# Mamba, attention and expert layers on one core: whole-row accumulations, a fifth slot for the products with B, gate column sums later

## Chip, cores and metric

The kernel runs on one core of one Trainium2 chip. The metric is the device time of a launch in microseconds (us), lower is better; the median of several runs counts.

## What is computed

The input is an image batch of 8 x 256 x 32 x 32, read as 8 sequences of 1024 tokens with 256 channels. Layer 0 is a Mamba block with a feed-forward part; layer 1 is attention with eight heads and a column bias from edges, then a mixture of experts; all in float32. What this case touches is the selective scan of layer 0 (d_inner 512, 16 states):

```python
xz = x @ W_in
xm, z = jnp.split(xz, 2, axis=-1)
...
xm = jax.nn.silu(xm)
dbl = xm @ W_x
dt, Bm, Cm = jnp.split(dbl, [dt_rank, dt_rank + d_state], axis=-1)
dt = jax.nn.softplus(dt @ W_dt + b_dt)
A = -jnp.exp(A_log)
def step(h, inputs):
    dt_t, B_t, C_t, x_t = inputs
    dA = jnp.exp(dt_t[..., None] * A)
    h = dA * h + (dt_t * x_t)[..., None] * B_t[:, None, :]
    y = jnp.einsum('bds,bs->bd', h, C_t)
    return (h, y)
...
y = ys.transpose(1, 0, 2) + xm * D_param
y = y * jax.nn.silu(z)
return y @ W_out
```

## The kernel before, in words

Each of the 8 sequences is cut into two chunks of 512 tokens, so there are 16 chunks, numbered 0 to 15. Even numbers are first chunks of a sequence (state zero at the start), odd ones are second chunks. The program is written as Python generators that emit instructions for the engines: TensorE (PE), VectorE (DVE), ScalarE (ACT), GpSimd (POOL) and SyncE (SP, which issues most DMAs). Every engine runs its own instructions in the order in which they were emitted.

The backbone is the loop at lines 2018 to 2051. It goes over 16 chunks x 32 steps = 512 groups. A group is one of 16 states (s) and one half (h, 256 of the 512 inner channels). For a group

- `decay` (line 763) has ScalarE compute exp(dt * A) into `da_all`, two groups ahead;
- `inputs` (line 780) takes a slot of `h4` and has DVE multiply x * dt by the row of B: hb, 128 x 1024;
- `scan` (line 791) has DVE run the recurrence along the tokens: one scan of 1024 in a first chunk (the decay of the second row's first column is set to zero), two of 512 with a starting state in a second chunk. In a first chunk POOL then copies the last column into `state`;
- `sums` (line 814) has DVE multiply hb by the row of C, and POOL issues a DMA that adds hb to the accumulator `dx` (`me["acc", h]`), which began as x * D. The slot comes free when that DMA has landed. In a first chunk multiply and DMA leave out the last column, because POOL's copy may still be reading it.

`h4` is a set of four slots (`H4` at line 263) of 4 KB a partition. The class `Slots` (line 275) hands out the slot that comes free first by the planner's own clock; the machine then waits for the true landing.

Around the backbone other streams are emitted by `advance` (line 1908), in an order of urgency: `prologue(i)` (line 561: load, layer norm, input product, convolution, dt), `park` (line 829: for chunks 2 to 15, layer norm and the gate z, both stored to DRAM), `gate_part` (line 852: brings silu(z) of a chunk back, as `sz`), `epilogue` (line 900: the gated y, the output product, the feed-forward part), then attention and the experts. `Model` (line 62) and the cost functions (lines 102 to 120) keep a running clock for each engine while the program is being written, and a stream is continued when its clock says that what it waits for is ready. `keep_warm` (line 1894) puts small filler products on PE where the model finds it idle. Tables give the moment of each start: `FRONT[i]` is the step of chunk i at which the prologue of i + 1 starts, `GATE[i]` that of its gate part; `CONV` and `SOFT` choose between forms of the convolution and of softplus (with `SOFT` 1, ScalarE and one more accumulating DMA do what a DVE instruction does otherwise; it doesn't act on chunk 0).

W_in is held as one tile `w_in` with 1024 columns: the first 512 give x, the rest z. `fold` (line 456) multiplies the columns by the layer norm's gain and makes the column sums of its shift. It is called for the x half in the head (line 1993), and for the z half by `setup` (line 1951), whose first piece is emitted at line 1991 while the loads are being issued.

At the end of a first chunk its last column has no term from C, since `sums` left it out. `epilogue` (lines 911 to 922) makes that term from `state` and C of the last token, and adds it to the accumulator's last column, ahead of the wait for the last accumulation to land (line 924).

Of the kernel before, what the change touches and what calls it, by code (L numbers as in the profile page):

```python
# [9 lines left out]
F32 = mybir.dt.float32  # L10
# [3 lines left out]
ALU = mybir.AluOpType  # L14
AX = mybir.AxisListType
PSUM = bass.MemoryType.PSUM

P = 128
B, C, L = 8, 256, 1024
KC = C // P  # L20
CH = 512
NCH = L // CH
DI, NS, RK, KW = 512, 16, 16, 4
ND = DI // P
HID = 1024
NH, HD = 8, 32
NPAIR = NH // 2
NHALF = ND // 2
# [26 lines left out]
def hybrid_kernel(ctx: ExitStack, tc: tile.TileContext, a: dict, out: bass.AP):  # L55
# [21 lines left out]
    model = Model()  # L77
# [58 lines left out]
    def load(name, shape, src):  # L136
        t = const.tile(shape, F32, name=name, tag=name)
        loads.append((t, src))
        return t
# [4 lines left out]
    def V(name, i=None, n=1):  # L144
        lo, hi = VEC[name]
        return vecs[:, lo:hi] if i is None else vecs[:, lo + i : lo + i + n]

    work = ctx.enter_context(ExitStack())
    work.enter_context(tc.manual_schedule(engines=set(ENGINES)))
    w_in = load("w_in", [P, KC, 2 * DI], a["W_in"].rearrange("(k p) n -> p k n", p=P))  # L150

    w_x = const.tile([P, ND, 4 * RK], F32, name="w_x")
    w_dt = const.tile([3 * RK, NHALF, P], F32, name="w_dt")
# [61 lines left out]
    taps = const.tile([P, ND * KW, HD], F32, name="taps")  # L215
    vec.memset(conv_tail, 0.0)
    b_in = const.tile([P, 2 * ND], F32, name="b_in")
    b1 = const.tile([P, HID // P], F32, name="b1")

    state = const.tile([P, NS, ND], F32, name="state")  # L220
    xsum = const.tile([P, KC, B, NCH], F32, name="xsum")
# [41 lines left out]
    T4, H4, PT, AHEAD, LAG, TICK = 25, 4, 4, 2, 8.0, 0.15  # L263


    FRONT = (7, 1, 1, 1, 1, 10, 16, 3, 14, 1, 10, 1, 13, 1, 13)
    GATE = (20, 7, 29, 25, 29, 21, 20, 15, 18, 30, 25, 28, 25, 14, 26, 15)
    CONV = (0, 0, 1, 1, 1, 1, 0, 0, 0, 0, 0, 0, 0, 0, 0, 0)
    SOFT = (0, 1, 1, 1, 1, 1, 0, 0, 0, 1, 0, 1, 1, 0, 1, 0)

    POLL, PARK = -1.0, 2
# [182 lines left out]
    def fold(w, n, gain, shift, bias, name, first=0):  # L456


        ps = sbank(f"{name}_{first}")
        cols = slice(first * P, (first + n) * P)  # L460
        for o in range(n):
            for k in range(KC):
                pe.matmul(
                    ps[:, o : o + 1], w[:, k, cols][:, o * P : (o + 1) * P], V(shift, k),
                    start=(k == 0), stop=(k == KC - 1),
                )
        yield
        if name == "b1":
            vec.tensor_tensor(bias, ps[:, :n], V("b1"), ALU.add)
        else:  # L470
            vec.tensor_copy(bias[:, first : first + n], ps[:, :n])
        for k in range(KC):
            vec.tensor_scalar(w[:, k, cols], w[:, k, cols], V(gain, k), None, ALU.mult)
# [87 lines left out]
    def prologue(i: int):  # L561
# [25 lines left out]
        def skip_path():  # L587

            for h in range(NHALF):
                dx = me["acc", h] = yield from mem.take(f"dx_{i}_{h}")  # L590
                for r in range(2):
                    act.activation(
                        dx[:, r, :], xm[h][:, r, :], AF.Identity, scale=V("D", 2 * h + r)
                    )

        if i == 0:
            yield from skip_path()
# [160 lines left out]
    def place(g):  # L758
        i, k = divmod(g, NSTEP)
        s, h = divmod(k, NHALF)  # L760
        return i, s, h
# [18 lines left out]
    def inputs(g):  # L780

        i, s, h = place(g)
        hb = hbs[g] = h4.now(f"hb_{g}")
        bc, landed = bcs[g // NHALF]
        vec.at = max(vec.at, landed)
        xd = chunk[i]["xd"][h]
        vec.tensor_tensor(hb, xd, bc[:, 0, :].unsqueeze(1).to_broadcast([P, 2, CH]), ALU.mult)
        if s == NS - 1:
            t4.put(xd)
# [24 lines left out]
    def sums(g):  # L814

        i, s, h = place(g)
        me = chunk[i]
        bc, _ = bcs[g // NHALF] if h < NHALF - 1 else bcs.pop(g // NHALF)
        hb = hbs.pop(g)
        n = CH if i % NCH == NCH - 1 else CH - 1  # L820
        y = hb[:, :, :n]
        vec.tensor_tensor(y, y, bc[:, 1, :n].unsqueeze(1).to_broadcast([P, 2, n]), ALU.mult)
        model.t = vec.at
        me["landed", h] = pool.dma_start(out=me["acc", h][:, :, :n], in_=y, accum_op=ALU.add)
        h4.put(hb, at=me["landed", h])

    parked = {}
# [1 line left out]
    def park():  # L829

        for i in range(PARK, B * NCH):
            b, c = divmod(i, NCH)
            xn_d = dram.tile([P, KC, CH], F32, name=f"xn_d_{i}", tag=f"xn_d_{i}")
            sz_d = dram.tile([NHALF, P, 2, CH], F32, name=f"sz_d_{i}", tag=f"sz_d_{i}")
            mem = Owner(t4, 3)
            xn = yield from mem.take(f"xe_{i}")
            yield sp.dma_start(xn, x_v[b, :, :, c * CH : (c + 1) * CH])
            yield from layernorm(mem, banks, xn, xn, f"a{i}")
            yield
            stored = sp.dma_start(xn_d, xn)  # L840
            sz = yield from gates(i, mem, xn)
            mem.put(xn, at=max(stored, model.end))
            for t in sz:
                act.activation(t, t, AF.Silu)
            lnexp()
            yield
            for h in range(NHALF):
                mem.put(sz[h], at=sp.dma_start(sz_d[h], sz[h]))
            mem.end()
            parked[i] = xn_d, sz_d  # L850

    def gate_part(i):

# [22 lines left out]
    def gates(i, mem, xn):  # L876

        while not gates_ready:
            yield POLL
        sz, ps = [], None  # L880
        for d in range(ND + 1):
            if d:
                h, q = divmod(d - 1, 2)
                act.activation(
                    sz[h][:, q, :], ps, AF.Identity, bias=b_in[:, ND + d - 1 : ND + d]
                )
                banks.put(ps)
            if d < ND:
                if d % 2 == 0:
                    sz.append((yield from mem.take(f"sz_{i}_{d // 2}")))  # L890
                ps = yield from banks.take(f"z_{i}_{d}")
                for k in range(KC):
                    pe.matmul(
                        ps, w_in[:, k, DI + d * P : DI + (d + 1) * P], xn[:, k, :],
                        start=(k == 0), stop=(k == KC - 1),
                    )
                yield
        return sz

    def epilogue(i: int):  # L900
# [9 lines left out]
        y = me["sz"]  # L910
        if c < NCH - 1:
            for h in range(NHALF):
                yl = work_pool.tile([P, NS + 1, 2], F32, name=f"yl_{i}_{h}", tag="yl")
                vec.tensor_tensor(
                    yl[:, 1:], state[:, :, 2 * h : 2 * h + 2],
                    me["c_last"].unsqueeze(2).to_broadcast([P, NS, 2]), ALU.mult,
                )
                vec.tensor_reduce(
                    yl[:, 0], yl[:, 1:].rearrange("p s d -> p d s"), AX.X, ALU.add
                )  # L920
                y_end = me["acc", h][:, :, CH - 1]
                vec.tensor_tensor(y_end, y_end, yl[:, 0], ALU.add)
        for h in range(NHALF):
            yield me["landed", h]
            vec.tensor_tensor(y[h], me["acc", h], y[h], ALU.mult)
            t4.put(me["acc", h])
        yield
# [932 lines left out]
    with tc.tile_pool(name="work", bufs=1) as work_pool:  # L1860
# [81 lines left out]
        def setup():  # L1942
            mem = Owner(t4, 9)
            tiles = []
            for n in range(9):
                tiles.append((yield from mem.take(f"setup_{n}")))
            held = []
            for n in range(2):
                held.append((yield from pairs.take(f"setup_p{n}")))
            pl = Scratch([t4.of[id(t)][1] for t in tiles])  # L1950
            yield from fold(w_in, ND, "ln1_g", "ln1_b", b_in, "b_in", ND)
            gates_ready.append(True)
            yield
            yield from column_bias(pl)
            yield
            eye = pl.tmp("eye", [P, P], F32)
            make_identity(nc, eye)
            blk = pl.tmp("eye_b", [P, HD], F32)
            yield
            for r in range(4):  # L1960
                rows = slice(HD * r, HD * r + HD)
                vec.tensor_copy(blk[rows, :], eye[rows, rows])
            vec.tensor_tensor(
                taps, blk.unsqueeze(1).to_broadcast([P, ND * KW, HD]),
                V("conv_w").unsqueeze(2).to_broadcast([P, ND * KW, HD]), ALU.mult,
            )
            set_up.append(True)
            yield
            yield from fold(w1, HID // P, "ln2_g", "ln2_b", b1, "b1")
            yield  # L1970
            yield from bounds(pl)
            yield
            yield from values_bias(pl)
            expert_constants(pl)
            mem.put(*tiles)
            mem.end()
            pairs.put(*held)
# [9 lines left out]
        next(first)  # L1987
        for n, (t, src) in enumerate(loads):
            sp.dma_start(t, src)
            if n == 2:  # L1990
                next(second)

        folding = fold(w_in, ND, "ln1_g", "ln1_b", b_in, "b_in")
        for n in range(8):
# [324 lines left out]
```

## Time and profile before

| what | value |
|---|---|
| median of 3 runs | 3440.32 us (3433.74 to 3444.18) |
| the profiled execution's own time | 3450.06 us |
| its span in the profile | 3448.1 us |
| DVE busy | 3031.7 us (88%) |
| PE busy | 3192.0 us (93%), filler included |
| ACT busy | 2459.8 us (71%) |
| accumulations of hb | 512 DMAs of 512 or 511 KB |
| DMA queue 0 (issued by POOL) | 138176 packets, 371.52 MB, 57.7% of 16 engines |

The profile names groups of instructions by what they write and read: `hb<-xm,bc` is the product with B, `hb<-da_all,hb` and `hb<-da_all,state,hb` are the scans, `hb<-hb,bc` is the product with C, `dx<-hb` is the accumulating DMA. Nearly all instructions carry line 98, the place where the planner emits them, so groups are told apart by their tiles. "Idle before" is time in which the engine stood still ahead of the instruction, with what ended it. DVE and ACT times can be added up; PE's busy time contains pipelined products.

### The profile page before, as it was taken

To read this page: it belongs to the slowest core of one execution; us is meant where nothing else is said; L and a number is where in the kernel's file an instruction comes from. 1 tells how busy PE (TensorE), PEld (TensorE's weight loads), DVE (VectorE), ACT (ScalarE), POOL (GpSimd) and SP (SyncE) were. 2 spreads that over 40 slices of the span, in tenths; PEclk is the share of its full clock that TensorE was granted. 3 is DMA by queue.
4 is the path that set the end of the run, shared out by engine and by line. 5 is a ranking of instruction groups with operands and counts; after the bars stand their busy time and mean duration, and the time that the engine had idled before them with its cause. 6 is when DMAs were issued, how large, how long until landed. Compare 5 with 4: busy or idle time off the path is not lost. (4 is left out here: it accounts for less than half of the span.)

```text
span 3448.1 us, 40234 instructions
## 1 busy us (share of the span) xinstructions
PE 3192.0 (93%) x14371; PEld 1355.8 (39%) x14371; DVE 3031.7 (88%) x3171; ACT 2459.8 (71%) x3550; POOL 1127.5 (33%) x1068
## 2 busy tenths in 40 slices
PE   7888889899999999999999998999999999999997
PEld 4544343433343334333443334334433343334343
DVE  5889999999999899999999999999999999972561
ACT  4665857578777887887778876887778768764643
POOL 0243224322542244233452244325542243311010
PEclk9889999899999999999999999999999999999999
DMA  3878999989998999898998989799889989971120
GB/s 105 222 170 204 213 224 214 226 206 228 196 206 185 210 203 218 181 210 198 228 207 188 221 196 222 187 215 207 193 189 209 202 191 199 225 160 61 32 77 23
DMA packets 233187, 642.22 MB, mean 186 GB/s; under 512 B 29520, under 2 KB 106000, under 8 KB 232976
## 3 DMA queue, kind: packets, MB, share of 16 engines
q0 software_dynamic: 138176, 371.52, 57.7%
q1 hardware_dynamic: 94800, 268.03, 23.5%
q8 instruction: 115, 1.88, 0.2%
q14 instruction: 96, 0.79, 0.1%
HBM read 253.33 MB, written 77.07 MB: 96 GB/s over the span
## 5 line engine op out<-in xcount | busy, mean ns | idle before, releaser
L95 POOL DMA_DIRECT2D dx<-hb x512 | 540.5, 1059 | 1567.2 <-DVE hb L98 1127.5
L98 ACT ACTIVATE da_all<-dt,vecs 128x512 f32<-128x512 f32 (+1 forms) x1024 | 698.1, 716 | 291.5 <-DVE hb L98 285.5
L98 DVE TENSOR_TENSOR hb<-xm,bc 128x1024 f32<-128x1024 f32 x512 | 617.0, 1205 | 28.1 <-DMA dx<-hb 27.5
L98 DVE TENSOR_TENSOR_SCAN hb<-da_all,state,hb 128x512 f32<-128x512 f32 x512 | 631.2, 1270 | 10.4 <-ACT da_all L98 10.4
L98 DVE TENSOR_TENSOR hb<-hb,bc 128x1024 f32<-128x1024 f32 (+1 forms) x512 | 624.9, 1220 | 0.0
L98 DVE TENSOR_TENSOR_SCAN hb<-da_all,hb 128x1024 f32<-128x1024 f32 x256 | 585.1, 2285 | 8.5 <-ACT da_all L98 8.5
L98 ACT ACTIVATE pt<-sc 128x1024 f32<-128x1024 f32 x512 | 494.2, 1017 | 84.3 <-PE sc L98 72.2
L98 POOL COPY state<-hb 128x2 f32<-128x2 f32 x256 | 339.3, 1332 | 238.1 <-DVE hb L98 211.0
L98 PE MATMUL warm<-mean_c,zero_c 128*128 128x256 f32 x1084 | 352.6, 446 | 63.6 <-ACT dt L98 13.8
L98 PE MATMUL sc<-qk,qk 32*128 32x512 f32 x2048 | 343.6, 644 | 21.9 <-ACT pt L98 18.2
L98 PEld LDWEIGHTS warm<-mean_c,zero_c 128*128 128x128 f32 x1084 | 205.7, 211 | 214.1 <-PE warm L98 80.5
L98 PE MATMUL num<-pt,v 128*32 128x512 f32 x2048 | 278.4, 614 | 11.9 <-DVE ot L98 11.8
L98 PE MATMUL fh<-x_f,w 128*128 128x512 f32 x480 | 232.4, 614 | 5.9 <-DVE x_f L98 3.2
L98 PE MATMUL den<-pt,ecb 128*32 128x512 f32 x1792 | 237.6, 601 | 0.0
L98 PE MATMUL facc<-fh,w 128*128 128x512 f32 x512 | 231.1, 598 | 5.4 <-ACT xp L98 1.7
L98 PE MATMUL re<-he,g 128*128 128x512 f32 x472 | 219.0, 609 | 6.5 <-ACT pt L98 2.3
L98 PE MATMUL he<-xe,g 128*128 128x512 f32 x448 | 217.6, 610 | 2.5 <-ACT he L98 2.2
L98 ACT ACT_TABLE_LOAD x159 | 204.0, 1283 | 3.5 <-PEq L2306 0.7
L98 PEld LDWEIGHTS sc<-qk,qk 32*128 32x128 f32 x2048 | 102.1, 183 | 211.9 <-ACT pt L98 93.0
L98 PEld LDWEIGHTS facc<-fh,w 128*128 128x128 f32 x512 | 95.0, 190 | 131.5 <-issue 118.8
L98 PEld LDWEIGHTS fh<-x_f,w 128*128 128x128 f32 x480 | 86.7, 192 | 138.3 <-issue 109.8
L98 PEld LDWEIGHTS re<-he,g 128*128 128x128 f32 x472 | 89.6, 195 | 126.5 <-issue 107.9
(376 smaller groups left out, 4326.7 us busy)
## 6 DMA issues: line engine op xcount, KB each, us to landing
bc<-bc_d SPq DMA_DIRECT2D x256, 512.0 KB, 4.9
dx<-hb POOLq DMA_DIRECT2D x256, 512.0 KB
dx<-hb POOLq DMA_DIRECT2D x256, 511.0 KB
dt<-e POOLq DMA_DIRECT2D x48, 512.0 KB
dt<-u POOLq DMA_DIRECT2D x30, 512.0 KB
sz_d<-sz SPq DMA_DIRECT2D x28, 512.0 KB, 4.4
sz<-sz_d SPq DMA_DIRECT2D x28, 512.0 KB, 11.4
xe<-xf_d SPq DMA_DIRECT2D x28, 512.0 KB
```

Source lines behind the costliest of these rows:

```text
L95: f(*args, **kw)
L98: return f(*args, **kw)
```

## The change

There are four edits.

1. W_in is loaded as two tiles, `w_in` for x and `w_z` for z, and the gate products and gate folding read `w_z`. The first piece of `setup` is no longer emitted among the loads; it comes with the rest of that stream. `b1` takes the place of its own input vector.
2. When all chunks have been parked and the gate parts of chunks 0 and 1 are done, `w_z` is no longer needed, and `park` adds its place to `h4` as a fifth slot. `inputs` now also moves the planner's clock to the moment at which a slot is free by the model.
3. In a first chunk the accumulating DMA takes the whole rows of hb, 512 columns. The multiply by C still leaves the last column out, so a sum that is not wanted goes into the accumulator's last column. That column is therefore written anew: ScalarE copies x * D of the column into a small tile in the prologue, DVE puts the term from `state` beside it, and after the last landing DVE writes the sum of the two.
4. The tables `FRONT`, `GATE` and `SOFT` have other values.

```diff
-    w_in = load("w_in", [P, KC, 2 * DI], a["W_in"].rearrange("(k p) n -> p k n", p=P))
+    w_in = load("w_in", [P, KC, DI], a["W_in"].rearrange("(k p) n -> p k n", p=P)[:, :, :DI])
+    w_z = load("w_z", [P, KC, DI], a["W_in"].rearrange("(k p) n -> p k n", p=P)[:, :, DI:])
...
-    b1 = const.tile([P, HID // P], F32, name="b1")
+    b1 = V("b1")
...
-    FRONT = (7, 1, 1, 1, 1, 10, 16, 3, 14, 1, 10, 1, 13, 1, 13)
-    GATE = (20, 7, 29, 25, 29, 21, 20, 15, 18, 30, 25, 28, 25, 14, 26, 15)
+    FRONT = (4, 1, 1, 1, 1, 10, 16, 1, 12, 2, 12, 3, 13, 9, 11)
+    GATE = (23, 8, 30, 29, 30, 27, 20, 23, 15, 30, 27, 24, 28, 16, 11, 10)
     CONV = (0, 0, 1, 1, 1, 1, 0, 0, 0, 0, 0, 0, 0, 0, 0, 0)
-    SOFT = (0, 1, 1, 1, 1, 1, 0, 0, 0, 1, 0, 1, 1, 0, 1, 0)
+    SOFT = (1, 1, 1, 0, 1, 1, 0, 0, 0, 1, 0, 1, 1, 0, 0, 1)
...
-        cols = slice(first * P, (first + n) * P)
+        cols = slice(0, n * P)
...
+                if c < NCH - 1:
+                    if h == 0:
+                        me["dx_end"] = work_pool.tile(
+                            [P, 2, NHALF, 2], F32, name=f"dxe_{i}", tag="dxe", bufs=2
+                        )
+                    act.copy(me["dx_end"][:, 0, h, :], dx[:, :, CH - 1])
...
     def inputs(g):
 
         i, s, h = place(g)
+        vec.at = max(vec.at, min(h4.free)[0])
         hb = hbs[g] = h4.now(f"hb_{g}")
...
-        me["landed", h] = pool.dma_start(out=me["acc", h][:, :, :n], in_=y, accum_op=ALU.add)
+        me["landed", h] = pool.dma_start(out=me["acc", h], in_=hb, accum_op=ALU.add)
...
+        while not {("g", i) for i in range(PARK)} <= done:
+            yield POLL
+        make = h4.make
+        h4.make = lambda nm, k: w_z if k == H4 else make(nm, k)
+        h4.free.append((model.t, H4))
...
                     pe.matmul(
-                        ps, w_in[:, k, DI + d * P : DI + (d + 1) * P], xn[:, k, :],
+                        ps, w_z[:, k, d * P : (d + 1) * P], xn[:, k, :],
...
-                yl = work_pool.tile([P, NS + 1, 2], F32, name=f"yl_{i}_{h}", tag="yl")
+                yl = work_pool.tile([P, NS, 2], F32, name=f"yl_{i}_{h}", tag="yl")
                 vec.tensor_tensor(
-                    yl[:, 1:], state[:, :, 2 * h : 2 * h + 2],
+                    yl, state[:, :, 2 * h : 2 * h + 2],
                     me["c_last"].unsqueeze(2).to_broadcast([P, NS, 2]), ALU.mult,
                 )
                 vec.tensor_reduce(
-                    yl[:, 0], yl[:, 1:].rearrange("p s d -> p d s"), AX.X, ALU.add
-                )
-                y_end = me["acc", h][:, :, CH - 1]
-                vec.tensor_tensor(y_end, y_end, yl[:, 0], ALU.add)
+                    me["dx_end"][:, 1, h], yl.rearrange("p s d -> p d s"), AX.X, ALU.add
+                )
         for h in range(NHALF):
             yield me["landed", h]
+            if c < NCH - 1:
+                vec.tensor_tensor(
+                    me["acc", h][:, :, CH - 1], me["dx_end"][:, 0, h], me["dx_end"][:, 1, h],
+                    ALU.add,
+                )
             vec.tensor_tensor(y[h], me["acc", h], y[h], ALU.mult)
...
-            yield from fold(w_in, ND, "ln1_g", "ln1_b", b_in, "b_in", ND)
+            yield from fold(w_z, ND, "ln1_g", "ln1_b", b_in, "b_in", ND)
...
             sp.dma_start(t, src)
-            if n == 2:
-                next(second)
```

## The prediction

> **What bounds the kernel now.** I read the page's busy shares and slices first, then the table of busy time by stage, then who waited for whom on VectorE (DVE), then its costliest groups.
>
> ```profile
> PE 3192.0 (93%) x14371; PEld 1355.8 (39%) x14371; DVE 3031.7 (88%) x3171; ACT 2459.8 (71%) x3550; POOL 1127.5 (33%) x1068
> ...
> DVE  5889999999999899999999999999999999972561
> ...
> DMA  3878999989998999898998989799889989971120
> ```
>
> DVE is at 9 from the fourth slice to the 36th and then falls off: the scan of the state holds the kernel for nine tenths of the time, and a stage without scans follows. TensorE (PE) looks busier, but part of it is filler: 1084 records of "warm" (352.6 us in the groups) and 272 of filler into open sums (76.8 us).
>
> ```profile
> 76.70:3072.00 2995.30, 2790.73 (x12627) 1168.04 (x12631) 2845.59 (x2816) 2252.01 (x3273) 1095.51 (x1020) 0.96 0.90 205
> 3072.00:3448.00 376.00, 347.21 (x1516) 153.68 (x1512) 149.91 (x292) 176.63 (x229) 30.29 (x32) 0.98 0.19 51
> ```
>
> The columns are window, length, then busy time of PE, PEld, DVE, ACT and POOL, the granted clock, the DMA share and GB/s. There are three stages: a head up to the first product of x and B at 76.7 us; the scan stage of 2995.3 us, in which DVE is busy 2845.6 and idle 149.7; a tail of 376 us that PE holds. Whatever the change gains in the scan stage must come out of those 149.7 us, or out of DVE's own work.
>
> ```profile
> DVE hb L98 <- DMA dx<-hb: 27.5, 18, 3.4
> DVE hb L98 <- ACT da_all L98: 18.9, 12, 4.1
> DVE tn_t L98 <- PE var_t L98: 17.5, 8, 4.1
> ...
> DVE sz L98 <- DMA dx<-hb: 4.6, 4, 1.8
> ```
>
> This is DVE's list of waits in the scan stage: total, times, longest. The first line is what the fifth slot aims at: a product of x and B waits until the accumulating transfer that last read its slot has landed, 18 times, 3.4 us at most. From 960 us on the same line says 23.7 us in 16 waits.
>
> ```profile
> L98 DVE TENSOR_TENSOR_SCAN hb<-da_all,state,hb 128x512 f32<-128x512 f32 x512 | 631.2, 1270 | 10.4 <-ACT da_all L98 10.4
> L98 DVE TENSOR_TENSOR hb<-xm,bc 128x1024 f32<-128x1024 f32 x512 | 617.0, 1205 | 28.1 <-DMA dx<-hb 27.5
> ```
>
> A group of a second chunk costs DVE 1.205 + 2 x 1.270 + 1.218 = 4.96 us; of a first chunk, with one scan of 2.285 us, 4.71 us.
>
> **What the skill says.** The Trainium skill, "DMA: Bandwidth & Descriptors", section "Anatomy of one DMA", says that the DMA engines do not wait on semaphores and that the issuing sequencer does. The trace agrees: POOL, which issues the accumulations, waited for an earlier one to land before it issued the next ("POOL dx <- DMA dx<-hb", 236.7 us in 59 waits), since two accumulations into one row must not overlap. The same page, "How a descriptor splits into AXI transactions", cuts a run into pieces of 256 B with a leftover; 2044 B is then 7 pieces and a leftover, so dropping one element saves nothing, while "Why small descriptors are slow" puts a fixed cost on every packet. The case's own numbers are below. "TensorE: Matmul & The Clock Gate", "What's actually happening", says that the array runs at half clock until it has been busy for a few microseconds. The trace agrees in the head, where weight loads for the 512-column product take 0.34 us at first and 0.19 us from 32 us on.
>
> **The change part by part.** The sum is made against the profiled execution, 3450.06 us (span 3448.1), 9.7 us above the median of the runs, 3440.32; I carry the difference over.
>
> *Gate column sums later (head).* Before the change PE's first instructions are the eight products for the gate half, which wait for all of W_in:
>
> ```profile
> 8.71 3.54 PE L98 MATMUL b_in<-vecs,w_in 128*128 128x1 f32 x16 [8.71 <-DMA w_in<-in_W_in]
> ...
> 12.12 3.76 PE L98 MATMUL mu_a<-xn,mean_c 128*128 128x512 f32 x4
> ```
>
> x was issued before W_in and has half its bytes; W_in's last byte is there at 8.7. In the changed program mu_a is PE's first instruction and waits for x alone. Issued at 1.19, x lands between 4.2 (3.0 us is the least from issue to landing that the view of this tile shows) and 8.7, so the head can lose 12.1 - 8.7 = 3.4 to 7.9 us. Against it: mu_a no longer follows 3.5 us of other products, so more of the 16 products of the convolution's input run at the slow rate (0.86 us apart against 0.43). Four more of them would be 1.7 us; the bound is all 16, 6.9 us, a loss. I take 4 us gained, from 3.5 lost (3.4 - 6.9) to 7.9 gained for the range. The gate sums move behind the input products, where fillers stand for about 10 us (36 records from 37.9): hidden; without that cover 3.5 us. The two loads instead of one add an issue of about 0.45 us on SP, ahead of small weights that PE needs only at 48 us: hidden.
>
> *Fifth slot.* The changed program uses it from group 121 of 512 (chunk 3), after all gate products, 79 times. In the old times that is at about 815 us, so it reaches nearly all of the 23.7 us. The longest of these waits is 3.4 us, and a fifth slot lets a transfer land one group (4.7 to 5.0 us) later: all would go. But where DVE comes 3 us earlier, ScalarE's decays can be late next (18.9 us now); I take 20 us, bounds 0 and 27.5: a slot more can't lengthen the wait for a slot. The planner's new line only moves its own clock up to the slot's; it adds no instruction.
>
> *Whole rows.* 256 accumulations go from 2 runs of 2044 B a partition to one of 4096 B. DMA queue rows of two neighbouring chunks, the first with the short rows:
>
> ```profile
> q0 software_dynamic: 9883, 21.49, 72.4%
> ```
> ```profile
> q0 software_dynamic: 6958, 23.54, 60.8%
> ```
>
> Share times window (167.5 and 200.7 us) times 16 engines over MB gives 90.3 and 82.9 engine-us per MB. Estimate from these: 256 x 0.52 MB x 7.4 / 16 = 62 us of each engine, some 8 us in each first chunk of about 187. DVE does not wait for bandwidth but for landings: beside the slots it waits 4.6 (sz) and 4.0 us (dt). I take 2 us gained, 0 to 8; a loss is excluded, as the same bytes and 0.2% more go in half the packets. The multiply stays at 511 columns, so no wait on POOL's copy of the state is added.
>
> *Last column.* DVE keeps its three small instructions per half and chunk (189, 188, 163 ns), 16 times each. The last of them moves behind the wait for the landing, where the gated product of 1217 ns waited anyway: two more small ones, about 0.2 us each, in 8 chunks stand between landing and product, 16 x 0.2 = 3 us at worst if nothing else fills them, and as much is saved earlier: 0. Behind that wait stand the scans of the next chunk, as before. ScalarE gets 16 copies of about 0.19 us, 3 us of an engine that is 71% busy: 0.
>
> *SOFT.* Among chunks 1 to 15 one fewer takes the path through ScalarE: DVE gains two instructions of 1222 ns, +2.4 us on the bound engine; ScalarE loses 2 x 1.05, POOL two accumulations.
>
> *FRONT and GATE.* They start the same work earlier or later: with a prologue move its load of xn on SP, its input products on PE and its accumulations on POOL; with a gate part the two 512 KB loads of sz on SP (most now start later, past loads of B and C). DVE's and PE's work besides is unchanged in count, and PE's work after the last chunk's output projection is the same list in both programs but for three fillers: the tail keeps its 376 us. What they do to the other 110 us of idle time in the scan stage has no row. Bounds: see the rivals. I take 0.
>
> Sum: -4 - 20 - 2 + 2.4 = -23.6: 3450.1 becomes 3426.5, the median 3440.3 becomes 3417.
>
> **The rivals.** *B, the gain is covered.* The slot's wait is only the front of a later one: accumulations into one half follow each other at landing, and ScalarE's decays stand close behind. Then DVE pays elsewhere what it saves; left are the head and SOFT, -4 + 2.4: 3438.7. For it: POOL's 236.7 us of waits for landings, which the fifth slot leaves. Against it: each half has two groups, 9.4 us or more, between accumulations, and the longest such POOL wait is 8.2.
>
> *C, the starts fit better.* In chunks 4, 6 and 8 DVE is idle 4.4, 4.2 and 3.9 us, over chunks 1 to 15 it is 127. If all were as chunk 4, that would be 66; three quarters of the 61, with head, SOFT and rows: -46 - 4 + 2.4 - 2 = -50: 3390. For it: waits on PE and ACT spread over many chunks. Against it: they have many causes.
>
> *D, slower: a chunk's dt comes late.* In the changed order the product of dt and x for chunks 11, 13 and 15 stands at groups 29 to 31, 29 to 31 and 28 to 30 of the chunk before, where it stood at 27 to 28, 25 to 26 and 26 to 28. DVE's queue is in order: if the chain of two accumulations before it is late, scans queue up behind it. At up to 8.2 us per landing, two landings at three places are 49 us: -24 + 49 = +25, 3465. It decides from 8 us per place, where the gain of 24 is gone. For it: "DVE xm <- DMA dt<-u" exists, 4.0 us in 2 waits. Against it: it is small even where chunks now stand at 31.
>
> **How the numbers follow.** Forecast 0.43 (3405 to 3430), B 0.19, C 0.18, D 0.20. About 0.3%, 10 us, is what a measurement of this kernel can tell from no change: faster, below 3430, is the forecast and C and a little of B: 0.62; same, B's rest, 0.18; slower, D, 0.20. The range reaches to C's number and to D's near end, 3388 to 3458, and leaves out half of each.
>
> **What would show it.** The first product of x and B starts at 71 to 74 us. DVE's wait for dx<-hb falls from 27.5 to under 8 us. Queue 0 has 32768 packets fewer for the accumulations. The tail stays 376 us within 5. I am wrong if DVE's idle time in the scan stage does not fall, or if "DVE xm" or "hb <- da_all" grow by what the slot gave.

## The result and the profile after

| what | before | after |
|---|---|---|
| median, same chip, 4 runs each | 3442.25 us | 3413.53 us (3409.81 to 3418.84) |
| ratio to before, 95% interval | 1 | 0.9922 [0.9899, 0.9944] |
| the profiled execution's own time, its span | 3450.06, 3448.1 us | 3418.84, 3416.5 us |
| head, up to the first product of x and B | 76.7 us | 71.9 us |
| scan stage, up to the end of the last product with C | 2991.3 us | 2966.1 us |
| tail | 380.0 us | 378.5 us |
| DVE idle, busy in the scan stage | 146.4, 2844.9 us | 120.7, 2845.4 us |
| all POOL time for issuing accumulations of hb | 540.5 us | 448.2 us |

The changed kernel is faster by 0.78%, some 27 us (0.0078 x 3442), between 19 and 35 us. The forecast was 23.6 us gained, 3417 us.

The page after has the same shape as before. The shares of the span, the slices and POOL's DMA queue are:

```profile
PE 3159.7 (92%) x14357; PEld 1346.3 (39%) x14357; DVE 3029.8 (89%) x3173; ACT 2455.3 (72%) x3564; POOL 1020.8 (30%) x1066
...
DVE  5989999999999899999999999999999999971661
...
DMA  3878999889897889798998988799889889861120
...
q0 software_dynamic: 105120, 370.73, 56.0%
```

DVE is at 9 in the slices from the fourth to the 35th, but for one 8, as it was before: the bound has not moved. POOL is busy 107 us less. The queue has 33056 packets fewer, of which 32768 are the accumulations that now go as one run, and its packets took 56.0% of 3416.5 us against 57.7% of 3448.1: 76 us less of each DMA engine. Not all of it is the rows' (see e7).

Busy time by stage, first before, then after. I set the end of the scan stage at the end of the last product with C here; the prediction's mark was 4 us later. The columns are window, length, PE, PEld, DVE, ACT and POOL busy, granted clock, DMA share and GB/s:

```profile
76.70:3068.00 2991.30, 2786.73 (x12595) 1166.36 (x12599) 2844.87 (x2813) 2248.28 (x3268) 1094.65 (x1019) 0.96 0.90 205
3068.00:3448.00 380.00, 351.21 (x1548) 155.36 (x1544) 150.64 (x294) 180.37 (x235) 31.14 (x33) 0.98 0.20 52
```
```profile
71.90:3038.00 2966.10, 2752.77 (x12586) 1157.82 (x12589) 2845.40 (x2820) 2246.69 (x3287) 988.91 (x1018) 0.97 0.89 207
3038.00:3416.50 378.50, 353.63 (x1542) 156.07 (x1533) 148.37 (x291) 177.27 (x228) 30.13 (x32) 0.98 0.18 50
```

Read across: DVE does the same work in the stage (2844.9 and 2845.4 us), and the stage is 25.2 us shorter. So the gain there is idle time, 146.4 down to 120.7. The head gave 4.8 and the tail 1.5.

Who DVE waited for in that stage after (total, times, longest):

```profile
DVE hb L98 <- ACT da_all L98: 15.9, 10, 3.7
DVE xm L98 <- DMA dt<-u: 9.2, 3, 5.9
...
DVE xf_x L98 <- PE mu_x L98: 4.7, 4, 2.1
...
DVE tn_t L98 <- PE mu_t L98: 3.4, 2, 2.7
DVE hb L98 <- DMA dx<-hb: 2.8, 2, 1.7
```

The wait for a slot, 27.5 us before, is 2.8 (the fifth slot's own products, named `w_z`, waited for no landing here). That is 24.7 us, and the idle time fell by 25.7. It looks as if the fifth slot had done all of it. The experiments show that this reading is wrong: a good part of the gain belongs to the whole rows, which do not appear under their name in this list.

### The profile page after: what moved, and what is told of

Same layout as the page of the kernel before. It is cut to its first block, busy times and chain, and to the rows that moved or that the text cites. A ratio compares the mean times of both kernels' runs of the same rounds, so it can differ in the third digit from the quotient of the medians.

```text
span 3416.5 us, 40186 instructions
## 1 busy us (share of the span) xinstructions
PE 3159.7 (92%) x14357; PEld 1346.3 (39%) x14357; DVE 3029.8 (89%) x3173; ACT 2455.3 (72%) x3564; POOL 1020.8 (30%) x1066
## 3 DMA queue, kind: packets, MB, share of 16 engines
q1 hardware_dynamic: 95072, 268.03, 23.6%
## 5 line engine op out<-in xcount | busy, mean ns | idle before, releaser
L95 POOL DMA_DIRECT2D dx<-hb x433 | 380.1, 880 | 1351.6 <-DVE hb L98 1006.4
L98 DVE TENSOR_TENSOR_SCAN hb<-da_all,state,hb 128x512 f32<-128x512 f32 x430 | 529.8, 1268 | 11.2 <-ACT da_all L98 11.2
L98 DVE TENSOR_TENSOR hb<-hb,bc 128x1022 f32<-128x1022 f32 (+1 forms) x433 | 528.0, 1219 | 0.0
L98 DVE TENSOR_TENSOR hb<-xm,bc 128x1024 f32<-128x1024 f32 x433 | 520.7, 1202 | 2.8 <-DMA dx<-hb 2.8
L98 DVE TENSOR_TENSOR_SCAN hb<-da_all,hb 128x1024 f32<-128x1024 f32 x218 | 497.9, 2284 | 4.7 <-ACT da_all L98 4.7
L98 PE MATMUL warm<-mean_c,zero_c 128*128 128x256 f32 x1118 | 336.9, 423 | 60.9 <-ACT dt L98 18.3
L98 POOL COPY state<-hb 128x2 f32<-128x2 f32 x218 | 256.2, 1177 | 261.7 <-DVE hb L98 249.0
L98 PE MATMUL xin<-xn,w_in 128*128 128x512 f32 x256 | 131.5, 644 | 19.0 <-ACT pt L98 7.3
```

Source lines behind the costliest of these rows:

```text
L95: f(*args, **kw)
L98: return f(*args, **kw)
```

## The experiments

Each ratio is that of a kernel to the kernel before on the same chip in five rounds, with its 95% interval; absolute times differ by some us from set to set (medians of the kernel before: 3451.7, 3441.1 and 3447.1 us). A step of 0.001 is 3.4 us. Head, stage and idle time come from the profile of one execution each, which can differ by a few us from the median.

### One part undone: e1, e2, e3

In all three the order of every instruction is that of the changed kernel; only the transfer's size or the place of hb differs. e1 has the short rows again:

```diff
-        me["landed", h] = pool.dma_start(out=me["acc", h], in_=hb, accum_op=ALU.add)
+        pool.at = max(pool.at, model.t) + 1.0
+        nc.gpsimd.dma_start(out=me["acc", h][:, :, :n], in_=y, accum_op=ALU.add)
+        me["landed", h] = model.move(pool.at, P * 2 * CH * 4, True)
```

> The changed kernel with one thing undone: in first chunks the accumulation takes 511 of the 512 columns again. Every engine's order and the last column's new form stay as they are in the changed kernel, and so does the planner's clock. Theory (the fifth slot and the head carry the gain, the rows little): 3414 to 3419 us, DVE's waits for dx<-hb stay under 8 us. Rival (the rows carry it: half the packets and, in the trace after, 0.86 us instead of up to 1.2 us of POOL per accumulation make landings earlier, so slots would have come free in time anyway): 3425 us or more, and DVE's waits for landings come back to over 15 us in the first chunks and those after them.

e2 has four places for hb:

```diff
+        h4.make = lambda nm, k: work_pool.tile([P, 2, CH], F32, name=nm, tag=f"h4_{g % H4}")
         hb = hbs[g] = h4.now(f"hb_{g}")
```

> The changed kernel with the same order on every engine and the same planner's clock, but the products with B go round four places instead of five; the fifth exists for the planner alone. Theory (the fifth slot takes about 20 us of waits away): 3433 us (3427 to 3440), and DVE's wait for dx<-hb ahead of hb<-xm,bc is back above 20 us. Rival (whole rows alone end those waits): 3414 to 3418 us, the waits under 8 us. Second rival (the order of the other work, from FRONT, GATE and the planner's new line, carries the gain): 3414 to 3418 us although the waits may come back.

e3 has both edits.

> The changed kernel with the same order on every engine, four places instead of five and 511 columns in first chunks, both as before. What is left of the change is the head, the last column, SOFT and the order. Theory: the slot's 20 us and the rows' 2 add: 3436 us (3430 to 3444). Rival (either alone is enough, they cover each other): the two undone one at a time cost nearly nothing, and together 20 us. Second rival (the order carries it): 3414 to 3420 us.

Measured: e1 0.9947 [0.9931, 0.9964], e2 0.9949 [0.9933, 0.9966], e3 0.9976 [0.9967, 0.9984]. Against the changed kernel's 0.9922 that is 9 us lost without whole rows, 9 us without the slot, 19 us without both. Counted from e3, the slot alone brings 10 us and the rows alone 9. So the two parts are worth about the same. The two from e3 are known to some 6 us either way, the two from the changed kernel to some 10, and the sum of both parts lies between 10 and 27 us. The theory of e1, which gave the rows 5 us at most, is out. So is that of e2, which gave the slot 20 us and expected its wait above 20 again. That of e3, 22 us for both, holds.

DVE's idle time in the stage says likewise, for one execution each: 150.1 us in e3, 131.9 in e1 (slot alone), 129.6 in e2 (rows alone), 120.7 with both. Here the first of the two takes 18 to 21 us and the second 9 to 11, so they may share some of the gain; the timed runs can't tell. In e3 the stage is

```profile
70.00:3067.60 2997.60, 2769.15 (x12585) 1163.37 (x12588) 2847.51 (x2820) 2246.49 (x3288) 1045.23 (x1018) 0.96 0.90 205
```

and the wait for a slot, in e3 first and then in e2,

```profile
DVE hb L98 <- DMA dx<-hb: 19.4, 14, 3.0
```
```profile
DVE hb L98 <- DMA dx<-hb: 14.2, 11, 2.9
```

The new order alone takes this wait from 27.5 to 19.4 us and the whole rows take it to 14.2, so the slot has only that left, of which it removes 11.4. Taken first, it removes 17.2: in e1, without the whole rows, the wait is 2.2 us. What a part is credited with depends on which comes first. And the short rows cost time in e1 without bringing that wait back.

### The two parts in the old order: e11

The kernel before, its order and tables kept instruction by instruction, but for the new form of the last column; the slot and the whole rows are added:

```diff
+        if len(places) == H4 and {("w",), ("g", 0), ("g", 1)} <= done:
+            places.insert(0, H4)
+        place_k = places.pop(0)
+        places.append(place_k)
+        h4.make = lambda nm, k: w_z if place_k == H4 else work_pool.tile(
+            [P, 2, CH], F32, name=nm, tag=f"h4_{place_k}"
+        )
         hb = hbs[g] = h4.now(f"hb_{g}")
...
-        me["landed", h] = pool.dma_start(out=me["acc", h][:, :, :n], in_=y, accum_op=ALU.add)
+        nc.gpsimd.dma_start(out=me["acc", h], in_=hb, accum_op=ALU.add)
```

> The kernel before with its own order of the work and its old tables, and two parts of the change alone: a fifth slot for the products with B (W_in's gate half as a tile of its own, used once all gate products and the first two gate parts are done) and whole rows in the first chunks, with the last column written anew. Nothing is left out. Theory that the two parts are worth some 9 us each whatever the order: ratio to the kernel before 0.994 to 0.9955, DVE idle in the scan stage 122 to 132 us against 146. Rival, that they pay only with the order and tables that were found for them: 0.998 to 1.000, idle above 140.

Measured: 0.9930 [0.9917, 0.9943], 24 us (20 to 29): a little more than the theory expected, and the rival is out. The stage and the slot's wait:

```profile
77.20:3044.40 2967.20, 2771.91 (x12595) 1161.73 (x12599) 2842.59 (x2813) 2247.35 (x3282) 998.81 (x1019) 0.97 0.89 207
```
```profile
DVE hb L98 <- DMA dx<-hb: 4.7, 4, 2.0
```

DVE's idle time is 124.6 us, 21.8 less than before, with the head where it was (77.2). The slot's wait alone is 22.8 us shorter, so here nearly all of the gain stands in that wait; which of the two parts brings it in the old order was not tried. Against the changed kernel's 0.9922 only 0.0008 is left for the new head, order and tables. e3, which has just these, gives 0.0024; the intervals hold both.

### The tables: e8 and e12

e8 is the changed kernel with the old tables, e12 the kernel before with the new ones:

```diff
-    FRONT = (7, 1, 1, 1, 1, 10, 16, 3, 14, 1, 10, 1, 13, 1, 13)
+    FRONT = (4, 1, 1, 1, 1, 10, 16, 1, 12, 2, 12, 3, 13, 9, 11)
...
```

(e12; `GATE` and `SOFT` likewise, and e8 the other way round.)

> The changed kernel with FRONT, GATE and SOFT as before; slot, rows, last column and head stay changed. The forecast gave the new tables 0 and SOFT +2.4 us, so: within 5 us of the changed kernel of this set, DVE busy about 2.4 us less. Rival (the tables were needed for the new parts to pay): 8 us or more slower, with more idle time on DVE at chunk ends.

> The kernel before with only the three tables FRONT, GATE and SOFT of the changed kernel; nothing is left out. Theory that a set of tables fits the program for which it was chosen and carries no gain of its own: slower than the kernel before by 10 to 60 us, ratio 1.003 to 1.017, as the changed kernel is with the old tables, with DVE's added idle time in a few chunks. Rival, that the new starts are better in themselves: 0.994 to 0.999.

Measured: e8 1.0077 [1.0055, 1.0098], e12 1.0128 [1.0112, 1.0144]. Each mixture is far slower than both kernels: e8 loses 53 us against the changed one, e12 loses 44 us against the one before. The stages of e8 and of e12:

```profile
72.90:3093.30 3020.40, 2784.86 (x12713) 1175.76 (x12717) 2847.28 (x2820) 2253.16 (x3293) 1007.17 (x1020) 0.96 0.87 204
```
```profile
74.70:3114.30 3039.60, 2799.78 (x12667) 1178.01 (x12671) 2849.23 (x2822) 2248.05 (x3274) 1059.97 (x1018) 0.96 0.89 202
```

The theory of e8 is out, its rival and the theory of e12 hold. DVE's work is the same within 5 us; its idle time is 173 and 190 us. In e8 these are among the longest of DVE's waits, and in e12 this one grew most (1.4 us before):

```profile
DVE xm L98 <- DMA dt<-e: 17.9, 4, 6.2
...
DVE xe L98 <- PE mu_a L98: 15.8, 4, 8.7
DVE xm L98 <- DMA dt<-u: 13.4, 5, 4.6
```
```profile
DVE xm L98 <- ACT dx L98: 15.5, 2, 11.3
```

The waits of xm are those of the next chunk's products for its dt and its x, behind which its scans queue up; the one of 11.3 us stands at the end of chunk 13 in e12. Waits of this kind (xm for dt<-e, dt<-u or dx) make about half of the added idle time: 29.5 of 52 us in e8, against the changed kernel, and 20.2 of 44 in e12, against the one before. That fits prologues which start too late in this order, or get too little done by then. e3 has the new tables too, with four places and short rows as in e12, and gives 0.9976: the tables are equal and the two parts absent in both, so the 52 us between them lie in the rest, for the most part probably in the order that the planner made (the head differs by 4.7 us in the traces, and e11 has the new form of the last column without a loss). Which of the planner's inputs makes the new tables fit was not tried (the fifth slot in its own clock, the clock line in `inputs` and the head all differ).

### The head: e4

`next(second)` is emitted among the loads again, in the changed kernel:

```diff
             sp.dma_start(t, src)
+            if n == 2:
+                next(second)
```

> The changed kernel with the gate column sums put back among the loads, ahead of PE's first layer norm product. The head's order is that of before, and the order of some later work moves a little with it. Theory: the head is 4 to 5 us longer (first product of x and B at 76 to 77 us instead of 71.9) and the kernel ends as much later: 3418 us (3414 to 3424). Rival (the head is taken up by a later wait, so that only scans start earlier): head longer, but 3411 to 3415 us.

Measured: 0.9910 [0.9892, 0.9929]: no loss, and neither the theory's longer head nor the rival's. PE's first instructions, in the changed kernel and then in e4:

```profile
6.41 3.75 PE L98 MATMUL mu_a<-xn,mean_c 128*128 128x512 f32 x4 [6.41 <-DMA xn<-in_x]
```
```profile
10.15 3.54 PE L98 MATMUL b_in<-vecs,w_z 128*128 128x1 f32 x16 [10.15 <-DMA w_dt<-in_W_dt]
13.56 3.66 PE L98 MATMUL mu_a<-xn,mean_c 128*128 128x512 f32 x4
```

The mean of x comes 7.1 us later in e4, and yet the first product of x and B is at 72.0 us, as after (71.9): the delay is 5.6 us at the end of the input product, 2.6 at the end of dt's product, and 0.1 at the first product with B. But the planner made another order there. In e4 the second product for the edge tables (`tt`) stands ahead of dt's product; in the changed kernel, as before, it stands behind. DVE's part of dt follows what waits for that product, and ScalarE waits for DVE, first in the changed kernel and then in e4:

```profile
57.68 1.06 ACT L98 ACTIVATE u<-u 128x1024 f32<-128x1024 f32 x1 [5.11 <-DVE e L98]
```
```profile
58.05 1.06 ACT L98 ACTIVATE u<-u 128x1024 f32<-128x1024 f32 x1 [1.29 <-DVE e L98]
```

So e4 does not isolate the early sums: what they cost is made up by another order behind them. The other traces tell more. The ten executions with the new head (after, e1 to e3 and e5 to e10) reach the first product with B at 69.0 to 72.9 us, 71.0 in the mean; the three with the old one at 76.7 (before), 77.2 (e11) and 74.7 (e12). The new head is about 5 us shorter. How much of that is the later gate sums, and whether it reaches the end of the kernel, no timed run shows.

### Where the rows pay: e5, e6, e7, e9

e5 is the changed kernel again, as a measure beside the next ones.

> The changed kernel itself, beside the next three on the same chip. Ratio to the kernel before 0.992 (0.989 to 0.995), as in its first measurement; DVE's idle time in the scan stage about 121 us.

Measured: 0.9925 [0.9905, 0.9945], idle 122.1 us: the same as the first time.

What does a short row cost? The trace of before shows two things: more packets, and a longer time on POOL. POOL's issues of the accumulations in most of chunk 2, with short rows, and most of chunk 3, with whole ones, both before:

```profile
L95 POOL DMA_DIRECT2D dx<-hb x31 | 36.6, 1182 | 70.5 <-DVE hb L98 46.4 <-DMA dx<-hb 12.7 <-issue 4.9
```
```profile
L95 POOL DMA_DIRECT2D dx<-hb x31 | 27.6, 892 | 130.3 <-DVE hb L98 93.2 <-DMA dx<-hb 19.4 <-DVE sq_a L98 7.2
```

By the median the issue takes 1.20 and 0.86 us. The Trainium skill, "Perfetto Trace Analysis", section "DMA Instruction — SWDGE (GPSIMD)", says that such a span ends when the last descriptor has been generated, not when the data has moved. The trace agrees: from the end of the issue to the last semaphore update of the landing another 6.6 us pass in the mean over first chunks, with short rows (before) and with whole ones (after).

e6 puts POOL time back, three memsets ahead of each first chunk's accumulation; e7 puts DMA time back, a copy of 64 KB from DRAM to DRAM by SP for each:

```diff
+        if n < CH:
+            for q in range(3):
+                nc.gpsimd.memset(spare[:, q : q + 1], 0.0)
```
```diff
+        if n < CH:
+            nc.sync.dma_start(junk_d[g], a["eW1"][:32, :])
```

> The changed kernel with three more memsets of one column, about 0.1 us each, on POOL ahead of each accumulation of a first chunk: POOL gets back the 0.33 us per accumulation that the whole rows took away (issue 1184 ns with 511 columns, 857 ns with 512), while the transfers keep their whole rows. All else, order and clock too, is as in the changed kernel. Theory now (the rows gain about 9 us through POOL: each accumulation is issued later, and POOL's queue and the next landing are later by as much): 8 to 11 us slower than the changed kernel of this set. Rival (the gain is in the DMA engines, which move half the packets): within 3 us of it.

> The changed kernel with one more DMA, 64 KB from DRAM to DRAM issued by SP beside each accumulation of a first chunk: the 16 DMA engines get back about the 4 engine-us per accumulation that the whole rows saved, as single reads of 2 KB rows and more at the utmost; POOL's issues keep their 857 ns. It computes nothing that is used. Rival (the rows gain through the DMA engines' time): 8 to 11 us slower than the changed kernel of this set. Theory (POOL's issue time): within 3 us of it.

Measured: e6 0.9923 [0.9904, 0.9943], e7 0.9934 [0.9910, 0.9957]. e6 tells nothing: the memsets ran while POOL was waiting for the product anyway. For e7, the DMA time that the rows save is read from POOL's queue in e1, which differs from the changed kernel in the rows alone:

```profile
q0 software_dynamic: 137888, 370.47, 57.7%
```

That is of 3424.1 us, against 56.0% of 3416.5: 62 us of each DMA engine. The copies of e7 put some 48 of them back (SP's queue is at 25.0% of 3415.0 us, in the changed kernel at 23.6%), and the mean DMA share of the first chunks 2 to 14 rose from 0.90 to 0.93. The kernel lost 3 us against e5 by the middle, but the two intervals allow up to 14, so the times don't exclude the DMA engines. The trace speaks against them: in the first chunks of e7 the accumulations land 7.0 us after the end of their issue, 7.9 after its start, as late as the short rows of e1 (7.8), and DVE's idle time is 123.5 us, near the 120.7 and 122.1 of the changed kernel.

e9 puts the POOL time where it counts, between the product and the issue, with a copy that itself waits for the product:

```diff
+        if n < CH:
+            nc.gpsimd.tensor_copy(spare[:, 0:1], hb[:, 0, 0:1])
```

> The changed kernel with one more instruction on POOL ahead of each of the 256 accumulations of a first chunk: a copy of one column of the product with C, which waits for that product, so that it costs POOL its time after the wait, between the end of the product and the issue of the accumulation. Same order of everything else; nothing is left out. Theory that whole rows pay through POOL's time between product and issue (0.34 us less for each issue): the accumulations and all that POOL issues behind them come later by what the copy takes, 0.2 to 1 us each, and most of the gain of the whole rows is gone: 6 to 15 us slower than the changed kernel, ratio to the kernel before 0.994 to 0.9965, DVE idle in the scan stage up from 121 to about 130 us or more. Rival, that POOL's time doesn't matter and whole rows pay through the transfer itself: within 3 us of the changed kernel, 0.9915 to 0.993.

Measured: 0.9955 [0.9943, 0.9967], 11 us slower than the changed kernel, inside what the POOL theory expected and outside the rival's. The copy took 1.7 us, five times what a short row adds, for a loss of about the same size, so the size alone proves little:

```profile
L834 POOL COPY spare<-hb 128x1 f32<-128x1 f32 x218 | 372.4, 1708 | 347.6 <-DVE hb L98 335.2 <-DVE yl L98 4.9 <-DVE s L98 3.5
```

But three of DVE's waits grew here as in e1; first e1, then e9:

```profile
DVE tn_t L98 <- PE mu_t L98: 8.1, 3, 3.4
DVE xf_x L98 <- PE mu_x L98: 7.3, 4, 3.1
...
DVE xm L98 <- DMA dt<-e: 2.2, 2, 1.5
```
```profile
DVE tn_t L98 <- PE mu_t L98: 8.8, 3, 3.6
...
DVE xf_x L98 <- PE mu_x L98: 7.0, 4, 3.4
...
DVE xm L98 <- DMA dt<-e: 3.5, 2, 2.5
```

Together 17.6 and 19.3 us. With whole rows these three waits make 8.1 us in the changed kernel, 6.0 in e2, and still 6.0 in e7, where DMA time was put back. What stands behind them are sums that POOL also issues as accumulating DMAs (`fo<-x1m_d`, `xr<-x_d`, `dt<-e`), in its queue behind the accumulations of hb. PE's own wait for the landing of the first two says likewise: 11.7 to 15.5 us in the six kernels of this order with whole rows (after, e2, e4 to e7; e10, with another queue of ScalarE, is left out), 20.1 in e1, 21.2 in e3 and 24.0 in e9. So a shorter issue lets these sums go earlier, and DVE waits less for dt and for the means that PE makes from the other two.

This is a part of the gain and not all of it. The waits for the variances, which follow those means, shrink where the waits for the means grow. With all waits of `tn_t`, `xf_x` and for dt<-e counted, it is 19.5 us in the changed kernel (17.1 to 22.0 in the six), 25.2 in e1 and 28.8 in e9: about half of the 11 and 18 us by which DVE's idle time grew. And in the old order PE waited only 1.5 us (before) and 1.8 (e11) for those sums, so there the rows have next to nothing to gain in this way. That the rows pay through POOL's queue in the new order is likely, then; that POOL's 0.34 us gives the full 9 us, and the DMA engines' time nothing, is not shown.

### POOL's other work: e10

If POOL's queue is what costs, the copies of the state might leave it. ACT makes them:

```diff
-            pool.tensor_copy(state[:, s, 2 * h : 2 * h + 2], hb[:, :, CH - 1])
+            pool.at = max(pool.at, model.t) + 1.2
+            model.end = max(model.end, pool.at)
+            nc.scalar.copy(state[:, s, 2 * h : 2 * h + 2], hb[:, :, CH - 1])
```

> The changed kernel with the 256 copies of a first chunk's last columns into the state moved from POOL (about 1.0 us each) to ACT (about 0.2 us each); nothing is left out. Theory that POOL's queue is what the first chunks wait for: POOL loses about 260 us of its 1020, DVE's waits in first chunks fall, 3 to 10 us faster than the changed kernel, 0.989 to 0.9915. Rival, that ACT's decays are the next thing late (DVE waits 16 us for them): the copy waits for the scan in ACT's queue, ahead of decays of later groups, and the kernel is slower than the changed one by 5 us or far more, with the growth in DVE's wait for da_all.

Measured: 1.0022 [1.0011, 1.0032], 34 us slower than the changed kernel. The theory had expected a gain and is wrong here; its rival holds in the time, though the wait for da_all is only 10 of the 33 us of added idle time. POOL lost 274 us of work, yet DVE's idle time is 154 us, with

```profile
DVE hb L98 <- ACT da_all L98: 25.8, 14, 3.6
DVE tn_t L98 <- PE var_t L98: 14.3, 8, 3.5
```

ACT's queue is in order too: each copy waits for a scan on DVE, and the decays and everything else of ACT wait behind it. In first chunks DVE's waits more than doubled (34 to 77 us, chunks 2 to 14).

## Why the prediction held, step by step

- *The sum.* -23.6 us was forecast, -27 (19 to 35) measured, and the mechanism is the one named: DVE's idle time falls, its work doesn't.
- *Slot and rows together.* -22 forecast; e11 gives -24 (20 to 29), e3 against the changed kernel -19 (10 to 27). This carries the forecast. That the sum came out is in part luck: the slot was priced some 10 us too high and the rows some 7 too low.
- *Fifth slot, -20.* Too large: about 10 (4 to 16). The wait fell by 20 and more, but not through the slot alone: by e3 the new order had taken 8 us of it, and by e2 the whole rows another 5. The step that failed is the one that took the whole wait of the old kernel as the slot's to remove, while other parts of the same change shorten the same wait. "ScalarE's decays can be late next" did not come true: their wait is 15.9 us with the changed kernel and 18.9 before.
- *Whole rows, -2.* Too small: about 9 (3 to 16), the middle past the bound of 8. The DMA engines' time was priced rightly, 62 us of each by the estimate and 62 by e1; the conclusion that DVE waits for landings and not for bandwidth is not contradicted by e7. What was left out is POOL: the 1059 ns of an issue stood in the groups as one mean, and split by chunk the medians are 1.20 and 0.86 us, 0.34 us x 256 = 88 us of an in-order queue. This is the term that was mis-sized; how much of the 9 us it carries stays open.
- *Cited rules.* The Trainium skill, "DMA: Bandwidth & Descriptors", section "Anatomy of one DMA", calls the generation of descriptors small and lets one emit a lot of them before it shows. Here twice the runs cost 1.20 us against 0.86, which is not small for this queue; the measurement stands. The pieces of 256 B in the prediction are stated for runs that start at a multiple of 256 B, and no run here shows them.
- *Head, -4.* 4.8 in the two profiles and about 5 over all of them. PE began with the mean of x at 6.4 us, between the 4.2 and 8.7 that were given; the input products kept their pace (9.8 us for 16, 9.9 before). The mechanism holds as far as the end of the head; what it is worth in the kernel's time was not measured.
- *SOFT, +2.4, and last column, 0.* DVE's work in the stage rose by 0.5 us. Both are too small to be told apart.
- *FRONT and GATE, 0.* Right only for the pair of new order and new tables: e3, the whole change without slot and rows, is 8 us faster than before (5 to 11), and its head is 6.7 us shorter in the trace. On their own the tables are worth +44 us (e12), and the old ones in the new program +53 (e8). A price of 0 for "starts earlier or later" was a guess that came out.
- *The tail.* Unchanged within 2 us, as forecast.
- *Rival B* (gain covered) is out: the idle time fell by as much as the slot's wait. *Rival C* (starts fit better) is out: e3 leaves idle time at 150.1 us. *Rival D* (dt late) did not decide: the wait of xm for dt<-u rose from 4.0 to 9.2 us, with 5.9 in one place, where it needed 8 at each of three. In e8 and e12 waits of its kind are about half of what made the kernel slower; so the danger was real, and it did not come with this pair of order and tables.
- *A misread line.* DVE's slices before are at 9 to the 35th and not the 36th, with an 8 in the 14th; nothing rests on it.

No run is faster than the changed kernel by more than the intervals.

## What to carry to other kernels

Where several parts of a change shorten the same wait, it can be credited once only: undo each part alone, in the same order, before you say which of them paid. When a DMA changes shape, price the issuing queue too (time of an issue, split by shape, and what else is issued behind it), and not the engines' bandwidth alone. Hand-tuned start tables belong to one order of the program; a variant that keeps the tables and changes the order measures the mismatch, so hold the order fixed to measure a mechanism, and compare the orders of two traces before you trust an edit that lets the planner run again (e4).

## What the hardware showed that I had not expected

- An accumulating DMA of 128 x 2 runs of 2044 B holds POOL for 1.20 us, one of 128 runs of 4096 B for 0.86 us (medians), while the time from there to landing is the same (6.6 us in the mean). Half the packets took 62 us less of each DMA engine's time.
- In e7 the same transfers landed 0.4 us later (7.0 us against 6.6), and DVE's idle time was 123.5 us, against 120.7 and 122.1 in two executions of the changed kernel.
- A copy of one column on POOL took 1.7 us on average in e9 (0.18 to 8.4), where copies of two columns took 1.0 (1.2 after): POOL's small copies are no cheap filler.
- The changed kernel's head ended at 71.9 us in one execution and at 69.0 in another. An edit of a few us there can't be judged from one profile of each kernel.
